# The end of a four-layer kernel: the last two chunks taken one by one instead of as a pair

## The chip, the cores and the metric

The kernel runs on one core of a Trainium2 chip. A core has TensorE (PE: matrix products and transposes, with its weight loads shown as PEld), VectorE (DVE), ScalarE (ACT), GpSimd (POOL), and SyncE (SP), which issues transfers. Each engine works through its own queue in order, and engines wait for one another through semaphores. PE writes its results to PSUM, eight banks of 512 floats in each of 128 partitions; the other engines copy them from there to SBUF. The metric is the device time in microseconds (us) of one execution.

## The reference

A stream x of 32 batches x 128 positions x 128 features goes through four blocks, each added to the stream: an attention of 16 heads of 64, a gated recurrence with a small coupling network, an attention of 16 heads of 8 behind a mixture of four experts (two chosen per batch), and last a slot network. The change is about this last block and about the end of the attention before it. Cut to what matters:

```python
out = attention(x) + x ; out = gamma * (out - mean) / sqrt(var + eps) + beta   # block 3, added to x
x1  = x + x @ layer_b                  # layer_b = base + rank-8 update of batch b
h   = gelu(x1 @ w1 + c)                # 128 -> 64 features
lg  = (h @ w2 + b2) / (|tau| + 0.1)    # 64 routes per position
alpha = softmax over the 8 highest of lg, 0 elsewhere
si  = alpha.T @ x1 / alpha.sum()       # 64 slots per batch
r, z, n = gates(si, slot_init) ; S = (1 - z) * n + z * slot_init
y   = layernorm(S + softmax(q(S) k(S).T) v(S))
x   = x + alpha @ (y @ wvp) @ wo
```

gelu here is the exact one; the gates use tanh.

## The kernel before, in words

The stream is held transposed in one SBUF tile X: features in partitions, 4096 positions in columns. A chunk is four batches (512 columns); there are eight chunks, 0 to 7, in four pairs. `col(g)` is chunk g of X.

Blocks 3 and 4 are written out by hand as a line of numbered steps (lines 1475 to 1508). Pair r has 24 steps of experts (k = 0 to 23) and then 8 of attention, so a pair takes TURN = 32 steps, and all four end at step 128 (END). Attention is itself a pipeline over batches: `advance` (line 1415) issues in one step the masks and scores of a batch, the weights of the batch before, the transposes of the one before that, and so on, so that a batch's result is added to R three steps after it came in, and its moments are taken four steps after. The last batch of chunk 6 comes in at step 122, that of chunk 7 at step 126; three further calls of `advance`, at steps 128 to 130, drain the pipeline.

Beside this line runs a plan. `at(i, f, *args)` (line 1343) enters a function for step i; `steps(i)` (line 1466) first takes every running generator one `yield` further, in the order in which they were started, and then starts what is planned for i. The block-4 functions for chunk g, with the number of steps that each runs over, are:

- `after_attention(g)` (1111, five steps): normalisation of R on ACT, transposes, X with gamma added; the product with lw (the per-batch layer) and xc = X + that product; for the second chunk of a pair the hidden product of both chunks into one PSUM bank (chunk a in partitions 0 to 63, chunk c in 64 to 127); and xn, the transpose of xc.
- `hidden(r)` (1147): one gelu over the pair's 128 partitions. `routes_top(g)` (1152): the w2 product, the logits lg and their eight highest on DVE. `routes_exp(r)` (1170): the exps of both chunks.
- `routes(g)` (1175, three steps): alpha, the slot inputs, their transposes. `slots_new(g)` (1210, six steps): gates with two tanh, the new slots sn, queries and keys, values, scores. `slots_exp(r)` (1263): the exps of the scores of both chunks.
- `slots_told(g)` (1267, eight steps): the slot attention's transposes, its weighted sum y, the normalisation of y, the transposes of y and the copy yT, the product with wvo, and the product with alpha that is added to ot, a transposed copy of `col(g)`; ot then goes to the output by a transfer on SP's queue (line 1331).

A pair's plan starts at t, the first step after its attention: `after_attention` at t and t + 3, `hidden` at t + 7, `routes_top` at t + 8 and t + 9, and so on to `slots_told` at t + 37 and t + 39, so the slots of a pair are told a full turn later, during the experts' steps of a following pair. For pair 3 (chunks 6 and 7) t is 128 and nothing else is left to run beside it except the telling of pair 2 (chunks 4 and 5), at steps 133 and 135.

What sets the order of instructions: `act(...)` (line 378) pins every ScalarE instruction behind all that is traced before it, so ScalarE keeps the order of the steps. PE, DVE and POOL instructions are pinned in the same way only inside `advance` (which, up to step 127, also calls `steps`); elsewhere a planner in the compiler orders them by when it reckons them ready, with the order of the steps as priority.

Two small supplies matter. From block 3 on, `ps()` (line 294) hands out only the three PSUM banks of the ring marked C; a bank is free again when its last reader is done. And ot, lw and the like share two buffers of 256 KB (tag h1): `layer_made(3)` puts the lw of chunks 6 and 7 there at step 116, and each is free after its product in `after_attention`.

## Time and profile before

| | |
|---|---|
| median of 3 runs | 1285.85 us (1284.26 to 1286.2) |
| profiled execution, own time | 1289.78 us |
| its span | 1288.0 us |
| its mean granted PE clock | 0.938 |
| PE, DVE, ACT, POOL busy | 88, 58, 57, 38 % |

The profile is of one execution. A row of a group tells busy time, mean length in nanoseconds and the idle time just before, with what ended it. A row of the timeline begins with its start in us from the start of the span and its length. Short instructions of one engine overlap a little, so lengths can add up to more than the time from first to last. The granted clock (PEclk) is a share of full speed; PE's own lengths follow it.

The end in numbers, from the timeline: chunk 7's last attention result is added to R until 1203.4; its X is ready at 1211.0 and its xc at 1213.9; the pair's gelu ends at 1219.2, the exps of both chunks' routes at 1236.9, chunk 7's new slots at 1257.5, and the last addition to ot at 1284.6. Chunks 4 and 5 have their last additions at 1230.5 and 1239.0, chunk 6 at 1278.9.

### The profile page before, as it was taken

The page shows a single profiled execution, that of the slowest core. Times are in us where ns is not written, and L with a number is a line of the kernel's source. Part 1 is how long each engine was busy: PE and PEld are TensorE (multiplying, and loading weights), DVE is VectorE, ACT ScalarE, POOL GpSimd, SP SyncE. Part 2 cuts the span into 40 slices and gives each one's busy share as a digit, 9 for nine tenths or more (in the row PEclk, how much of TensorE's full clock was granted, in tenths as well). Part 3 has the DMA queues.
Part 4 walks back from the last instruction along what each step waited for, and adds up shares of the span by engine and source line. Part 5 has one row for each costly group of instructions (what it writes and reads, how often), then busy time and mean ns, then how long its engine had stood idle before and what let it go on. Part 6 is the DMA issues. An engine that isn't in the chain of part 4 may idle for free. (4 is left out here: it accounts for less than half of the span.)

```text
span 1288.0 us, 24292 instructions
## 1 busy us (share of the span) xinstructions
PE 1131.8 (88%) x9509; PEld 714.9 (56%) x9509; DVE 749.1 (58%) x1996; ACT 738.3 (57%) x1857; POOL 490.2 (38%) x433
## 2 busy tenths in 40 slices
PE   4999899989999899899887777998999899989765
PEld 1565555535555355555454445676776677667543
DVE  1354848465584655936736468555756674667454
ACT  1756565655656656554355555665875587558421
POOL 1555655446555555534345532123213321222000
PEclk9999999999999999889888898999999999999765
DMA  6000000000000000000231210144023502220000
GB/s 259 1 1 2 1 2 1 1 1 1 1 1 1 1 1 2 1 1 1 93 113 53 84 57 10 41 134 132 11 75 92 155 11 75 91 65 11 2 17 17
DMA packets 18322, 51.99 MB, mean 40 GB/s; under 512 B 1568, under 2 KB 7840, under 8 KB 17952
## 3 DMA queue, kind: packets, MB, share of 16 engines
q0 software_dynamic: 9648, 40.01, 10.0%
q1 hardware_dynamic: 7984, 9.38, 2.3%
q8 instruction: 75, 1.23, 0.4%
q10 hardware_dynamic: 576, 1.05, 0.2%
q14 instruction: 39, 0.32, 0.1%
HBM read 46.25 MB, written 2.10 MB: 38 GB/s over the span
## 5 line engine op out<-in xcount | busy, mean ns | idle before, releaser
L380 ACT ACTIVATE s_sb<-ps,s_max 128x128 f32<-128x128 f32 x512 | 139.2, 383 | 132.3 <-DVE s_max L256 125.9
L256 POOL TENSOR_TENSOR s_sb<-s_sb,s_sum 128x1024 f32<-128x1024 f32 (+1 forms) x64 | 119.7, 1871 | 76.7 <-DVE s_sum L256 58.0
L256 PE MATMUL ps<-hT,w_attn 128*128 128x512 f32 x256 | 126.6, 625 | 11.2 <-DVE hT L256 11.2
L256 POOL TENSOR_TENSOR s_half<-s_sb 128x512 f32<-128x512 f32 x62 | 79.5, 1282 | 110.6 <-ACT s_sb L380 110.5
L256 POOL DMA_INDIRECT ew<-in_expert,rows x64 | 64.4, 1006 | 127.4 <-DVE ye L256 79.4
L380 ACT ACTIVATE qk<-ps 128x512 f32<-128x512 f32 x128 | 74.4, 615 | 64.2 <-PE ps L256 63.7
L256 DVE TENSOR_REDUCE s_max<-ps 128x4 f32<-128x512 f32 x128 | 81.2, 673 | 51.1 <-PE ps L256 51.0
L380 ACT ACT_TABLE_LOAD x61 | 78.3, 1283 | 53.4 <-DVE s_max L256 38.9
L256 DVE TENSOR_REDUCE s_sum<-s_half 128x8 f32<-128x256 f32 x62 | 25.7, 415 | 121.8 <-POOL s_half L256 121.8
L256 PEld LDWEIGHTS ps<-qk 64*128 64x128 f32 x1024 | 66.9, 193 | 38.0 <-issue 38.0
L256 PEld LDWEIGHTS ps<-hT,w_attn 128*128 128x128 f32 x256 | 47.9, 197 | 71.4 <-issue 49.1
L380 ACT ACTIVATE he<-ps,ew 128x128 f32<-128x128 f32 x256 | 71.3, 386 | 26.3 <-issue 19.2
L380 ACT ACTIVATE s<-ps,s1max 128x128 f32<-128x128 f32 x256 | 73.1, 390 | 19.3 <-DVE s1max L256 19.3
L256 PEld LDWEIGHTS ps<-he,ew 128*128 128x128 f32 x512 | 68.2, 198 | 26.3 <-ACT he L380 14.2
L256 PE MATMUL ps<-he,ew 128*128 128x128 f32 x512 | 77.1, 292 | 6.2 <-ACT he L380 5.2
L256 PE MATMUL ps<-qk 64*128 64x128 f32 x1024 | 80.4, 292 | 0.0
L256 PE MATMUL ps<-w_base,s_sb 128*128 128x128 f32 x512 | 75.0, 291 | 3.6 <-ACT s_sb L380 2.7
L256 PE MATMUL ps<-pT,v 128*64 128x128 f32 x1024 | 73.0, 287 | 5.2 <-DVE X L256 2.5
L256 PE MATMUL ps<-X,ew 128*128 128x128 f32 x512 | 76.1, 282 | 0.4 <-DMA ew<-in_expert,rows 0.4
L256 DVE TENSOR_REDUCE s1m<-ps 128x6 f32<-128x384 f32 x128 | 64.9, 547 | 17.6 <-PE ps L256 17.6
L256 PEld LDWEIGHTS ps<-X,ew 128*128 128x128 f32 x512 | 66.7, 193 | 10.6 <-issue 9.0
L256 PE MATMUL ps<-w_base,s 128*128 128x128 f32 x384 | 62.2, 288 | 7.9 <-ACT s L380 4.8
(298 smaller groups left out, 2427.5 us busy)
## 6 DMA issues: line engine op xcount, KB each, us to landing
v1o<-v SPq DMA_DIRECT2D x8, 256.0 KB, 3.5
out_x<-ot SPq DMA_DIRECT2D x8, 256.0 KB, 2.3
X<-in_xT ACTq DMA_DIRECT2D x4, 256.0 KB, 7.0
X<-in_xT SPq DMA_DIRECT2D x4, 256.0 KB, 9.4
w_attn<-in_attn POOLq DMA_DIRECT2D x1, 1024.0 KB
w_lowr<-in_lowr SPq DMA_DIRECT2D x1, 1024.0 KB, 12.6
ew<-in_expert,rows POOLq DMA_INDIRECT x64, 5.4
w_ffn<-in_ffn SPq DMA_DIRECT2D x1, 928.0 KB, 10.5
```

The costliest lines, as they stand in the source:

```text
L256: ins = f(*args, **kwargs)
L380: return tc.keep_in_program_order(A.activation(*args, **kwargs))
```

## The change

Three things are changed in the plan and two functions get a form for one chunk.

1. Pair 3 is planned chunk by chunk. Chunk 6 starts at step 126 and chunk 7 at step 130, and each runs on its own: `after_attention(g, True)` makes the hidden product of that chunk alone in partitions 0 to 63, `hidden_alone` takes its gelu, and the later functions follow at +6 (`routes_top`), +7, +8, +11, +16 and +17 (`slots_told`). Chunk 6's `slots_told` so begins at step 143 and chunk 7's at 147, where they began at 165 and 167.
2. The telling of pair 2 begins at step 127 for chunk 4 and 131 for chunk 5, where it began at 133 and 135. The telling of pairs 0 and 1 keeps its steps.
3. In `slots_told`, for every chunk, the four transposes of the stream and their copy to ot stand ahead of the weighted sum, three `yield`s before the transposes of y, behind which they stood.

`routes_exp` and `slots_exp` take chunks instead of a pair. Nothing is computed differently but for the split gelu.

```diff
-    def after_attention(g):
+    def after_attention(g, alone=False):
...
-        if g % 2:
+        if alone:
+            HSs[g, 0] = ps()
+            mm(HSs[g, 0][:NS], w("f_w1a"), xc)
+        elif g % 2:
             HSs[g // 2] = ps()
...
+    def hidden_alone(g):
+        p = HSs[g, 0]
+        HSs[g, 0] = mpool.tile([P, CH], F32, tag="h2", name="hs", bufs=1)
+        act(HSs[g, 0][:NS], p[:NS], AF.Gelu, bias=cb1[:NS])
...
     def routes_top(g):
-        e = slice(g % 2 * NS, g % 2 * NS + NS)
-        hs = HSs[g // 2]
+        alone = (g, 0) in HSs
+        e = slice(0, NS) if alone else slice(g % 2 * NS, g % 2 * NS + NS)
+        hs = HSs[g, 0] if alone else HSs[g // 2]
...
-    def routes_exp(r):
-        for g in (2 * r, 2 * r + 1):
+    def routes_exp(*gs):
+        for g in gs:
...
-    def slots_exp(r):
-        for g in (2 * r, 2 * r + 1):
+    def slots_exp(*gs):
+        for g in gs:
...
         act(y, p[:, 2 * D :].rearrange("p (q d) -> p q d", d=D), AF.Copy)
         yield
+
+        ot = mpool.tile([P, CB, D], F32, tag="h1", name="ot")
+        p4 = ps()
+        for b in range(CB):
+            T.transpose(p4[:, bass.ts(b, S)], col(g)[:, bass.ts(b, S)], ident)
+        act(ot, b3(p4), AF.Copy)
         p = ps()
...
             T.transpose(p[:, bass.ts(q, P)], y[:, q, :], ident)
-
-        ot = mpool.tile([P, CB, D], F32, tag="h1", name="ot")
-        p4 = ps()
-        for b in range(CB):
-            T.transpose(p4[:, bass.ts(b, S)], col(g)[:, bass.ts(b, S)], ident)
-        act(ot, b3(p4), AF.Copy)
...
+        if r == NP - 1:
+
+            for g, n in ((a, t - 2), (c, t + 2)):
+                at(n, after_attention, g, True)
+                at(n + 5, hidden_alone, g)
+                at(n + 6, routes_top, g)
+                at(n + 7, routes_exp, g)
+                at(n + 8, routes, g)
+                at(n + 11, slots_new, g)
+                at(n + 16, slots_exp, g)
+                at(n + 17, slots_told, g)
+            continue
...
-        at(t + 25, slots_exp, r)
-        at(t + TURN + 5, slots_told, a)
-        at(t + TURN + 7, slots_told, c)
+        at(t + 25, slots_exp, a, c)
+        t += TURN + 5 if r < NP - 2 else TURN - 1
+        at(t, slots_told, a)
+        at(t + (2 if r < NP - 2 else 4), slots_told, c)
```

More of the change, by code (lines that the diff above doesn't have):

```diff
@@ L1404, in program @@
         at(t + 9, routes_top, c)
-        at(t + 12, routes_exp, r)
+        at(t + 12, routes_exp, a, c)
         at(t + 13, routes, a)
```

## The prediction

> **What bounds the kernel now.** I read the page's slices first, then stretches of the end, then ScalarE's own order of instructions there, then the timeline around each of its waits.

> ```profile
> span 1288.0 us, 24292 instructions
> ...
> PE   4999899989999899899887777998999899989765
> ...
> PEclk9999999999999999889888898999999999999765
> ```

> TensorE (PE) is nearly full until the last three slices of 32.2 us. There it is 70, 60 and 50 per cent busy and its granted clock falls too. That is the only stretch the change works on in earnest. Cut at seven places of the timeline:

> ```profile
> core 0: us, PE busy (x) PEld busy (x) DVE busy (x) ACT busy (x) POOL busy (x), PEclk, DMA share, GB/s
> 1184.03:1189.42 5.39, 5.09 (x132) 3.93 (x128) 4.87 (x22) 4.64 (x13) 1.11 (x2) 1.00 0.01 3
> 1194.90:1203.46 8.56, 7.63 (x152) 5.85 (x150) 2.17 (x8) 5.16 (x11) 1.29 (x3) 0.80 0.01 3
> 1203.46:1213.86 10.40, 6.71 (x28) 4.87 (x28) 5.80 (x22) 2.13 (x5) 0.00 (x0) 0.61 0.00 1
> 1213.86:1219.16 5.30, 3.78 (x21) 1.56 (x20) 1.84 (x11) 3.21 (x5) 0.00 (x0) 0.80 0.00 0
> 1219.16:1236.91 17.75, 11.74 (x55) 9.47 (x56) 11.58 (x66) 4.75 (x9) 0.00 (x0) 0.51 0.05 16
> 1236.91:1257.54 20.63, 12.63 (x64) 7.80 (x64) 10.70 (x33) 4.45 (x11) 0.00 (x0) 0.67 0.05 14
> 1257.54:1288.00 30.46, 17.19 (x80) 10.85 (x80) 11.30 (x54) 4.83 (x12) 0.00 (x0) 0.50 0.06 17
> ```

> The first row is one full attention step (5.4 us, PE 94 per cent busy, full clock). The others are the end: attention draining (chunk 7's last result at 1203.4), chunk 7's xc, the gelu, both exps of the routes, chunk 7's new slots, and the output. No engine is full after 1203: it is a chain of hand-overs. ScalarE (ACT) keeps the order in which the code writes it, and two of its waits are that order alone:

> ```profile
> 1228.21 0.41 DVE L256 TENSOR_TENSOR lg<-lg,m 128x256 f32<-128x256 f32 x1
> ...
> 1233.83 0.60 ACT L380 ACTIVATE ot<-ps 128x512 f32<-128x512 f32 x1 [7.27 <-PE ps L256]
> 1234.32 0.56 ACT L380 ACTIVATE yT<-ps,w_base 128x256 f32<-128x256 f32 x1
> 1234.90 1.28 ACT L380 ACT_TABLE_LOAD   x1
> ...
> 1236.19 0.72 ACT L380 ACTIVATE lg<-lg 128x256 f32<-128x256 f32 x2
> ...
> 1250.45 0.48 DVE L256 SCALAR_TENSOR_TENSOR n<-ps,w_base,rz 128x256 f32<-128x256 f32 x1
> ...
> 1252.96 0.46 ACT L380 ACTIVATE slot_qk<-ps,w_base 32x256 f32<-32x256 f32 x1 [2.51 <-PE ps L256]
> 1254.85 0.46 ACT L380 ACTIVATE slot_qk<-ps,w_base 32x256 f32<-32x256 f32 x1 [1.42 <-PE ps L256]
> 1255.22 0.40 ACT L380 ACTIVATE n<-n 128x256 f32<-128x256 f32 x1
> ```

> Both logits are ready at 1228.6, but the exps stand behind chunk 5's ot and yT and begin at 1236.2: 7.6 us. Chunk 7's n is ready at 1250.9 and its tanh waits until 1255.2 behind chunk 6's queries and keys: 4.3 us.

> **The parts of the change.** I follow chunk 7, which ends last, with PE durations as they stand at half clock.

> *Drain.* In steps 126 to 129 ACT gets R of chunk 6 (1.64 us) and chunk 4's sl_pT and y (0.38 + 0.36) among its last attention work. ACT has idle gaps of 1.19, 0.42, 0.19 and 1.19 there, so I give this nothing; behind them in its queue stands attention's last copy oS. DVE gets chunk 4's three short normalisations (0.7 us in 1194.9 to 1203.4, where it is 2.17 of 8.56 busy), POOL the memset of xn, and POOL has no other work after 1203. PE gets chunk 6's R transposes (1.1) and chunk 4's four transposes (1.27) ahead of the last values, because attention's instructions are pinned behind all that is traced before them: +2.4 (0 if the gaps hold it, 3.5 if ACT's work sticks out).

> *Up to xc.* Traced ahead of it on PE: of chunk 6 the lw product 2.1, its own hidden product 1.0 (half of the pair's 1.98), xc transposes 1.1, w2 product 1.85; of chunk 4 stream transposes 1.1, weighted sum 1.12, y 0.69, wvo 1.23; of chunk 5 1.26. Together 11.45. The row of 10.40 us leaves 6.7 beside chunk 7's own R transposes and lw product (1.63 + 2.1), so 4.7 sticks out. Lower bound 0 (the planner puts it behind), upper 8.5 (only the 3.0 of others' work done there now is hidden). I take +4.7, as PE's order follows program order when several are ready.

> *To the gelu,* now 5.30. One hidden product less: -1.0. ACT now writes gelu(6), exp(6), gelu(7), exp(7): four tables in place of two. [...] Gelu(7) also stands behind alT of chunk 6: exp 0.38, products 1.35, transposes 0.69, copy 0.38 make 2.8, about half of it while chunk 7's xc is transposed: +1.4 (0 to 2.8). Behind this gelu stand yT of chunk 5 and siT of chunk 6, which then come late for chunk 5's output and chunk 6's gates, not for chunk 7. Together +3.0.

> *To the exp,* now 17.75. What is left: w2 product 1.85, one logit group on DVE 3.4 (0.48 + 4 x 0.52 + 2 x 0.42), chunk 5's normalisation in between 1.8, exp 0.38, no ot or yT left in front: 7.4, so **-10.3**. The table load is hidden behind the logits.

> Up to the exp: 2.4 + 4.7 + 3.0 - 10.3 = -0.2. The wait of 7.6 us is paid back before it is reached.

> *Exp to new slots,* now 20.63. Chunk 7's own path is alpha 1.35, product 1.13, division 0.75, transposes 0.66, copy 0.38, gates 1.13 + 0.4 + 0.63 + 0.85 + 0.42, slots 1.2, hand-overs 0.7: 9.6. Chunk 6, four steps ahead, puts its queries, keys and values before the gates (1.06 + 1.06 + 2.1) and about 1.0 of DVE: 14.8, so -5.8. The tanh no longer stands behind queries (4.3 of it).

> *New slots to the end,* now 27.1 to the last addition. The own path is 17.7. On top: chunk 6's stream transposes and weighted sum 2.2, its y, wvo and output products 3.1, own stream transposes 1.1, half of chunk 6's normalisation 1.8: 25.9, so -1.2. The stream's move is in this: now the copy to ot stands right before yT,

> ```profile
> 1279.73 0.60 ACT L380 ACTIVATE ot<-ps 128x512 f32<-128x512 f32 x1 [4.74 <-PE ps L256]
> 1280.22 0.56 ACT L380 ACTIVATE yT<-ps,w_base 128x256 f32<-128x256 f32 x1
> ```

> though y's transposes end at 1278.6: 1.6 us, gone in the new order. The tile ot is taken while both lw of pair 3 are alive in the same two buffers, so chunk 5's copy waits for chunk 7's lw product and exp(6) stands behind it. Nothing late: by the sum exp(6)'s logits come no sooner. The output DMA of chunks 4 and 5 moves with it; SP has nothing behind it (0.38 us each, landing in 2.3).

> *Left out so far.* ps() has three banks here. Chunk 7's hidden product holds one until its gelu ends, 8.2 us by the sum where the pair's held it 5.3 (1213.9 to 1219.2), and two serve the rest: +1.2 (0 to 2.9). Laying the same rows out in the old order ends 1.3 us short of the trace: +1.3.

> *The six earlier chunks* get only the stream's move, in stretches where PE is 95 to 99 per cent busy: the same four transposes and one copy of 0.6 us, three slots earlier. Nothing; at most 0.5 us a pair either way.

> **Sum:** -0.2 - 5.8 - 1.2 + 2.5 = -4.7 us. The profiled execution took 1289.78 (its span 1288.0 and 1.78 around it), 3.93 above the median of the runs; I take the difference off the median: 1285.85 - 4.7 = **1281.1 us**. A difference under 0.2 per cent (2.6 us) counts as none.

> **Rivals.**

> *Slower: ACT's order, chunk 7's gelu behind chunk 6's exp.* From chunk 6's last logit operation to the end of gelu(7) ACT's order needs table 1.28, exp 0.38, alpha 1.35, transposes 0.69, alT 0.38, table 1.28, gelu 0.69: 6.1. My sum puts that gelu at 1229.2, so it stands with the logits at 1223.1. Now the first are done at 1225.9 and share DVE with chunks 4 and 5. Break-even is 1227.8; at 1232 the kernel is 4.2 us slower: **1290**. For it: three chunks stand before them on PE. Against: R of chunk 6 can start 6 us sooner (1195.5 for 1201.4).

> *No difference:* the exp is no earlier, and chunk 6's work, four steps ahead, only changes places with its old self before chunk 7: **1285.5**. [...]

> [...]

> **How the numbers follow.** My sum (1279 to 1283.5 as its own range): 0.40; clock 0.18; no difference 0.20; slower 0.22. Of my case 0.36 lies beyond 0.2 per cent and 0.04 within; of no difference 0.01 falls out on the slow side: faster 0.54, same 0.23, slower 0.23. Of the clock case the part under 1272, of the slower one the part over 1291, is left out, under 2 in 10: 1272 to 1291.

> **What would show it.** Right: exp(6) straight after its own logits, without ot and yT of chunk 5 before it; four table loads after 1199; xc of chunk 7 some 7 us later than 1213.9; tanh of n within 0.3 us of its n; yT not behind ot at the very end. Wrong: attention's last result later than 1208; gelu(7) later than 1234; a granted clock above 0.7 from 1203 to 1240; PE waits for banks over 3 us; or a change of over 2 us before 1184.

## The result, and the profile after

The changed kernel takes **1275.28 us** (median of 4 runs, 1274.24 to 1276.74) against 1286.03 (1284.26 to 1286.23) for the kernel before: a ratio of 0.9923, 95% interval 0.9911 to 0.9936, so 8.2 to 11.4 us less. The forecast was 1281.1: the direction was right and the time lies inside the range of 1272 to 1291, but the gain is more than twice the forecast one. It lies outside the sum's own range of 1279 to 1283.5: the wide range holds it only because the 1274 us of the rival called clock, an estimate of mine, had pulled its lower end down. The profiled execution took 1274.46 us, 0.8 below its median, where that of before was 3.8 above its own.

First the page of the kernel after, its slices.

```profile
span 1272.7 us, 24291 instructions
...
PE   3999899989989899899887767899899989998774
...
PEclk9999999999999989989898989999999999999867
```

Up to the last three slices nothing is different in kind; the end goes from 7, 6, 5 tenths of PE to 7, 7, 4. Now the end, cut at the same events as before the change (a full attention step; attention's last result to chunk 7's xc; to the gelu's end; to chunk 7's exp; to its new slots; to the end of the span). The columns are the stretch, its length, each engine's busy time with the number of its instructions, the granted PE clock, and transfers.

```profile
core 0: us, PE busy (x) PEld busy (x) DVE busy (x) ACT busy (x) POOL busy (x), PEclk, DMA share, GB/s
1178.10:1183.47 5.37, 5.09 (x132) 3.94 (x128) 4.57 (x19) 4.64 (x13) 1.11 (x2) 1.00 0.01 3
...
1198.92:1213.12 14.20, 10.34 (x49) 7.92 (x48) 8.83 (x55) 5.90 (x11) 0.00 (x0) 0.67 0.01 2
1213.12:1222.07 8.95, 5.31 (x37) 2.96 (x36) 6.23 (x30) 5.24 (x8) 0.00 (x0) 0.88 0.09 29
1222.07:1228.86 6.79, 6.52 (x26) 5.03 (x26) 4.07 (x20) 2.42 (x5) 0.00 (x0) 0.58 0.00 0
1228.86:1245.86 17.00, 10.60 (x43) 5.52 (x42) 8.89 (x26) 3.78 (x10) 0.00 (x0) 0.67 0.05 16
1245.86:1272.70 26.84, 12.71 (x76) 8.80 (x76) 11.33 (x51) 4.83 (x11) 0.00 (x0) 0.69 0.07 20
```

The stretch to xc has grown from 10.40 to 14.20 us and the one to the gelu from 5.30 to 8.95; the one from the gelu to the exp has shrunk from 17.75 to 6.79. After it, 20.63 became 17.00 and 30.46 became 26.84. The sign of every stretch is the forecast's. ScalarE's own order shows why; this is its timeline in the kernel after (start, length, instruction, in brackets the wait before it).

```profile
1213.28 0.60 ACT L380 ACTIVATE ot<-ps 128x512 f32<-128x512 f32 x1 [4.90 <-PE ps L256]
1213.90 1.28 ACT L380 ACT_TABLE_LOAD   x1
1215.19 0.42 ACT L380 ACTIVATE lg<-lg 128x256 f32<-128x256 f32 x1
1216.56 0.60 ACT L380 ACTIVATE xn<-ps 128x512 f32<-128x512 f32 x1 [0.95 <-PE ps L256]
1219.69 0.38 ACT L380 ACTIVATE alT<-ps 128x256 f32<-128x256 f32 x1 [2.54 <-PE ps L256]
1220.09 1.28 ACT L380 ACT_TABLE_LOAD   x1
1221.39 0.68 ACT L380 ACTIVATE hs<-ps,cb 64x512 f32<-64x512 f32 x1
1221.97 0.55 ACT L380 ACTIVATE yT<-ps,w_base 128x256 f32<-128x256 f32 x1
1222.42 0.37 ACT L380 ACTIVATE siT<-ps 128x256 f32<-128x256 f32 x1
1222.81 1.28 ACT L380 ACT_TABLE_LOAD   x1
1228.44 0.42 ACT L380 ACTIVATE lg<-lg 128x256 f32<-128x256 f32 x1 [4.35 <-DVE lg L256]
...
1264.93 0.56 ACT L380 ACTIVATE yT<-ps,w_base 128x256 f32<-128x256 f32 x1 [5.61 <-PE ps L256]
```

The last step of each chunk's logits on DVE and, further on, chunk 7's n with its tanh:

```profile
1214.72 0.42 DVE L256 TENSOR_TENSOR lg<-lg,m 128x256 f32<-128x256 f32 x1
...
1227.99 0.41 DVE L256 TENSOR_TENSOR lg<-lg,m 128x256 f32<-128x256 f32 x1
...
1243.41 0.48 DVE L256 SCALAR_TENSOR_TENSOR n<-ps,w_base,rz 128x256 f32<-128x256 f32 x1
...
1243.93 0.42 ACT L380 ACTIVATE n<-n 128x256 f32<-128x256 f32 x1 [0.89 <-DVE n L256]
```

And ScalarE's group of table loads after 1193.6 (line, engine, operation, count; busy, mean ns; idle before):

```profile
L380 ACT ACT_TABLE_LOAD x4 | 5.1, 1283 | 0.1
```

The same row of before, after 1199, from which the forecast took 2.57 us for two more loads:

```profile
L380 ACT ACT_TABLE_LOAD x2 | 2.6, 1283 | 0.0
```

Each exp now begins as soon as its own logits are there: chunk 6's at 1215.19 (logits done at 1215.14), chunk 7's at 1228.44 (1228.40). The ot and yT of chunk 5 have not left ScalarE's order: its ot still stands right ahead of chunk 6's exp, as the prediction said of the tile ot, and its yT ahead of chunk 7's. But both are done before those logits are. Chunk 6's table load ends 0.04 us after its logits, chunk 7's long before; in the kernel before, the exps began 7.6 us after both logits were ready. Chunk 7's gelu (hs at 1221.39) stands behind chunk 6's alT and a table load. At the very end yT waits for PE alone. The loads are four, with next to no idle time ahead of them.

The two profiled executions do not begin the end at the same time: attention's last transfer of v1o is issued at 1168.0 before and 1162.1 after, though 2.7 of these 5.9 us are there at the first one (702.0 and 699.3), before any changed instruction. I therefore count everything below from that last transfer. From it to the end of the span it is **120.0 us before and 110.6 after, 9.4 less**, which the interval above holds.

### The profile page after: what moved, and what is told of

Its sections match the earlier page's. It is cut to its first block, busy times and chain, and to the rows that moved or that the text cites. A ratio compares the mean times of both kernels' runs of the same rounds, so it can differ in the third digit from the quotient of the medians.

```text
span 1272.7 us, 24291 instructions
## 1 busy us (share of the span) xinstructions
PE 1119.8 (88%) x9509; PEld 708.1 (56%) x9509; DVE 749.9 (59%) x1996; ACT 741.9 (58%) x1860; POOL 488.6 (38%) x433
## 3 DMA queue, kind: packets, MB, share of 16 engines
q8 instruction: 75, 1.23, 0.4%
## 5 line engine op out<-in xcount | busy, mean ns | idle before, releaser
L380 ACT ACTIVATE s_sb<-ps,s_max 128x128 f32<-128x128 f32 x512 | 139.2, 383 | 132.6 <-DVE s_max L256 126.3
L256 POOL TENSOR_TENSOR s_sb<-s_sb,s_sum 128x1024 f32<-128x1024 f32 (+1 forms) x64 | 119.7, 1871 | 76.6 <-DVE s_sum L256 58.0
L256 PE MATMUL ps<-hT,w_attn 128*128 128x512 f32 x256 | 126.4, 623 | 11.7 <-DVE hT L256 11.3
L256 POOL TENSOR_TENSOR s_half<-s_sb 128x512 f32<-128x512 f32 x62 | 79.5, 1282 | 108.5 <-ACT s_sb L380 108.4
L256 POOL DMA_INDIRECT ew<-in_expert,rows x64 | 63.5, 992 | 129.2 <-DVE ye L256 79.3
L380 ACT ACT_TABLE_LOAD x63 | 80.8, 1283 | 52.5 <-DVE s_max L256 38.9
L380 ACT ACTIVATE qk<-ps 128x512 f32<-128x512 f32 x128 | 74.4, 616 | 61.5 <-PE ps L256 60.9
L256 DVE TENSOR_REDUCE s_max<-ps 128x4 f32<-128x512 f32 x128 | 81.1, 673 | 48.2 <-PE ps L256 48.0
L256 DVE TENSOR_REDUCE s_sum<-s_half 128x8 f32<-128x256 f32 x62 | 25.7, 415 | 122.1 <-POOL s_half L256 122.1
L380 ACT ACTIVATE he<-ps,ew 128x128 f32<-128x128 f32 x256 | 71.6, 385 | 32.3 <-issue 19.0
L256 PEld LDWEIGHTS ps<-hT,w_attn 128*128 128x128 f32 x256 | 47.5, 196 | 71.7 <-issue 48.4
L256 PEld LDWEIGHTS ps<-qk 64*128 64x128 f32 x1024 | 66.2, 190 | 36.9 <-issue 36.9
L380 ACT ACTIVATE s<-ps,s1max 128x128 f32<-128x128 f32 x256 | 73.1, 390 | 19.7 <-DVE s1max L256 19.6
L256 PE MATMUL ps<-he,ew 128*128 128x128 f32 x512 | 76.3, 289 | 5.4 <-ACT he L380 4.6
L256 PEld LDWEIGHTS ps<-he,ew 128*128 128x128 f32 x512 | 67.1, 195 | 24.3 <-ACT he L380 12.4
L256 PE MATMUL ps<-qk 64*128 64x128 f32 x1024 | 79.6, 289 | 0.0
L256 PE MATMUL ps<-pT,v 128*64 128x128 f32 x1024 | 72.7, 286 | 5.3 <-DVE X L256 2.5
L256 PE MATMUL ps<-w_base,s_sb 128*128 128x128 f32 x512 | 74.2, 289 | 3.6 <-ACT s_sb L380 2.7
L256 PE MATMUL ps<-X,ew 128*128 128x128 f32 x512 | 76.6, 281 | 0.4 <-DMA ew<-in_expert,rows 0.4
L256 DVE TENSOR_REDUCE s1m<-ps 128x6 f32<-128x384 f32 x128 | 64.9, 547 | 16.3 <-PE ps L256 16.3
L256 PEld LDWEIGHTS ps<-X,ew 128*128 128x128 f32 x512 | 66.8, 192 | 10.9 <-issue 9.2
L256 PE MATMUL ps<-w_base,s 128*128 128x128 f32 x384 | 62.1, 288 | 7.9 <-ACT s L380 4.8
```

The costliest lines, as they stand in the source:

```text
L256: ins = f(*args, **kwargs)
L380: return tc.keep_in_program_order(A.activation(*args, **kwargs))
```

## The experiments

The theory after the result: it is the change of order, with exps that no longer wait for chunk 5 as its core. Rivals: PE's clock (0.50 in the last stretch before, 0.69 after), or one part alone, or something ahead of the end.

**The parts by themselves.** e1 does only the move of the stream's transposes and ot. e2 does only the earlier telling of chunks 4 and 5:

```diff
-        at(t + TURN + 5, slots_told, a)
-        at(t + TURN + 7, slots_told, c)
+        t += TURN + 5 if r != NP - 2 else TURN - 1
+        at(t, slots_told, a)
+        at(t + (2 if r != NP - 2 else 4), slots_told, c)
```

e3 is the changed kernel with ot's four transposes and copy put back:

```diff
         yield
-        ot = mpool.tile([P, CB, D], F32, tag="h1", name="ot")
-        p4 = ps()
-        for b in range(CB):
-            T.transpose(p4[:, bass.ts(b, S)], col(g)[:, bass.ts(b, S)], ident)
-        act(ot, b3(p4), AF.Copy)
         p = ps()
...
             T.transpose(p[:, bass.ts(q, P)], y[:, q, :], ident)
+        ot = mpool.tile([P, CB, D], F32, tag="h1", name="ot")
+        p4 = ps()
+        for b in range(CB):
+            T.transpose(p4[:, bass.ts(b, S)], col(g)[:, bass.ts(b, S)], ident)
+        act(ot, b3(p4), AF.Copy)
```

> Only the stream's transposes and the copy to ot go two steps sooner; the last pair stays together and slots_told stay at their old steps. My account: at the very end ot no longer stands right before yT (1.6 us between the end of y's transposes and yT's start in the profile of before), but chunk 5's ot still stands with yT before the exps, so about 1284.3 us, -1.6 us. If the tile ot makes the early copy wait for chunk 7's lw product and exp behind it, 1285 to 1288. If the move changes the six earlier chunks (1.4 us of the whole gain lie outside the last stretch in the two medians), 1282.9 or less with the first changed attention step already earlier in the trace. If it is off the path, 1285.9.

> Only slots_told of chunks 4 and 5 go into the attention's drain (steps 127 and 131); the last pair stays together and the stream's transposes stay where they were. My account: ot and yT of chunk 5 are gone from in front of the exps (7.6 us), while PE gets four to five us of their work ahead of chunk 7's xc: about 1282.5 us, -3.4. If this part carries the whole gain and the split only changes places, 1276 to 1278. If the work only shifts in front of xc one for one, 1285.9. With the exps 7.6 us sooner and nothing paid, 1278.3.

> The whole change without its last part: the stream's transposes and the copy to ot are back after y's transposes, right before yT. My account: ot before yT costs 1.6 us at the end of chunk 7, so 1276.9 us (1.6 above the changed kernel). If the early copy to ot made exp(6) wait for its tile, the time is equal to or under the changed kernel's 1275.3. If the stream's move gave nothing, 1275.3.

| kernel | ratio to before, 95% | last v1o to end | change | last stretch (new slots to last addition), its clock |
|---|---|---|---|---|
| before | 1 | 120.0 | | 27.10, 0.50 |
| e1, stream alone | 0.9966 (0.9951 to 0.9981) | 117.6 | -2.4 | 24.84, 0.50 |
| e2, telling alone | 0.9963 (0.9949 to 0.9977) | 116.9 | -3.1 | 27.07, 0.50 |
| e3, all but the stream | 0.9939 (0.9923 to 0.9956) | 113.9 | -6.1 | 26.45, 0.50 |
| after | 0.9923 (0.9911 to 0.9936) | 110.6 | -9.4 | 23.49, 0.72 |

No part carries it alone: telling gives 3.1, the split on top of it 3.0 (6.1 less 3.1), the stream on top of both 3.3 (9.4 less 6.1), or 2.4 by itself. The split without the earlier telling was not tried. A trace shows one execution, and those of before, e1, e2 and e3 took 2 to 3.8 us more than their medians. By the ratios e1, e2 and e3 gain more, 4.4, 4.8 and 7.8 us of the whole 9.9; the stream's move on top of the rest, 2.1 by them, is not clear of noise. By either count no single part makes the whole.

e2 shows the exps by themselves, and what the split is for. With the pair together and only the telling earlier, chunk 5's ot and yT stand in a stretch in which the logits are not ready, and each exp waits for DVE:

```profile
1222.12 0.59 ACT L380 ACTIVATE ot<-ps 128x512 f32<-128x512 f32 x1
1222.60 0.57 ACT L380 ACTIVATE yT<-ps,w_base 128x256 f32<-128x256 f32 x1
...
1227.47 0.42 ACT L380 ACTIVATE lg<-lg 128x256 f32<-128x256 f32 x1 [3.01 <-DVE lg L256]
1230.11 0.42 ACT L380 ACTIVATE lg<-lg 128x256 f32<-128x256 f32 x1 [2.22 <-DVE lg L256]
```

The exps end at 63.2 and 65.8 us from the last v1o transfer (before: 68.9 for the later), but chunk 7's new slots come only 3.1 us sooner. From its exp to its new slots it takes 20.65 us, as before (20.63), where e3 with the split takes 16.61: together, both chunks go through the gates side by side.

e1 gave 2.4 in its trace where I had expected 1.6, e2 3.1 where I had expected 3.4, and what e3 lacks reads 3.3, again for 1.6. Of these, e1's is the clean one, because the last stretch ran at the same clock in both kernels. These are the rows of that stretch, first before, then e1:

```profile
1257.54:1284.64 27.10, 17.19 (x80) 10.85 (x80) 11.30 (x54) 4.83 (x12) 0.00 (x0) 0.50 0.03 10
```

```profile
1254.39:1279.23 24.84, 16.85 (x80) 11.07 (x80) 11.22 (x54) 5.05 (x12) 0.00 (x0) 0.50 0.03 11
```

and these of e3 and of e10 (below), whose last stretch has the changed kernel's order:

```profile
1252.44:1278.89 26.45, 15.55 (x76) 10.52 (x76) 11.44 (x51) 4.52 (x11) 0.00 (x0) 0.50 0.04 11
```

```profile
1244.93:1270.59 25.66, 14.81 (x76) 9.80 (x76) 11.44 (x51) 4.85 (x11) 0.00 (x0) 0.57 0.04 11
```

At 0.57 the new order takes 25.66 (25.62 and 25.69 in e11 and e4, also at 0.57) against 23.49 at 0.72. So of the 3.0 us between e3's 26.45 and the 23.49 after, some 2.2 go with the clock and at most 0.8 with ot's place, since 0.50 and 0.57 are not the same clock either.

**Is it the clock?** The means of the stretches above, 0.58 to 0.88, hide how the clock ran. Cut at its own steps, the kernel after shows this (same columns as before):

```profile
1207.28:1210.69 3.41, 3.41 (x15) 3.01 (x14) 0.48 (x1) 0.97 (x3) 0.00 (x0) 0.50 0.02 5
1210.69:1214.11 3.42, 3.42 (x20) 2.87 (x19) 2.73 (x15) 0.81 (x2) 0.00 (x0) 0.50 0.00 0
1214.11:1217.52 3.41, 2.41 (x16) 1.13 (x14) 3.03 (x14) 2.08 (x3) 0.00 (x0) 1.00 0.19 61
1217.52:1220.93 3.41, 1.83 (x14) 1.10 (x14) 2.86 (x16) 1.22 (x2) 0.00 (x0) 1.00 0.05 16
1220.93:1224.35 3.42, 2.31 (x10) 2.11 (x10) 0.23 (x1) 3.13 (x5) 0.00 (x0) 0.50 0.00 0
1224.35:1227.76 3.41, 3.41 (x16) 2.58 (x15) 2.75 (x17) 0.00 (x0) 0.00 (x0) 0.50 0.00 0
1227.76:1231.17 3.41, 0.91 (x6) 0.34 (x4) 3.30 (x10) 0.94 (x2) 0.00 (x0) 1.00 0.25 77
```

Here it is 1.00 or 0.50, for whole windows of 3.41 us. Half clock gave way to full at 1214.11 after two windows of half clock with PE full (3.42 of 3.42 us in the second), and at 1227.76 after one (3.41 of 3.41); the window at full clock from 1217.52, with 1.83 us busy, was followed by half. So I tried to hold it up, with products that nobody reads. e4 puts 16 ahead of y's transposes in the last two chunks:

```diff
+        if g >= NCH - 2:
+            spare = bank("A")
+            for _ in range(16):
+                mm(spare[:, 0 : 2 * P], ident16, twice16.rearrange("p u t -> p (u t)"))
```

> The changed kernel with 16 idle products (128x256, bf16, into a spare bank, nobody reads them) while y of chunks 6 and 7 is normalised, where PE waits 4.1 us each time. It tells what the granted clock is worth: the end runs at 0.69 of full clock with PE 12.7 us busy of 26.9. If the low clock follows from PE's pauses and prices the end, 0.69 goes to 0.85 or more behind the filler and PE's own 12.7 us shrink by 2 us: 1273.3. If the clock does not answer to so short a filler, or its products reach past the wait: 1275.3 to 1277.

The ratio is 0.9932 (0.9909 to 0.9956), no different from the changed kernel. The products did not stay where I wrote them. They read only constants, nothing pins them, and the trace has all 32 between 1189.8 and 1203.7, in attention's drain. There they held the clock at 1.00, and chunk 7's xc stands at 49.3 us from the last v1o transfer in place of 51.0, but the last stretch ran at 0.57. The run says nothing of idle products at the end. e6 and e7 pin them, and spread them over the waits:

```diff
+    def idle(n):
+        if late:                       # from step 131
+            spare = bank("A")
+            pinned.append(True)
+            for _ in range(n):
+                mm(spare[:, 0 : 2 * P], ident16, twice16.rearrange("p u t -> p (u t)"))
+            pinned.pop()
...
+        idle(20)   # ahead of y's transposes; 10 ahead of xn's products and of sl_s's
+                   # transposes, 5 ahead of the w2 products and of the first slot products
```

e6 is this on the changed kernel, e7 on the kernel before; e5 is the changed kernel once more, beside them.

> The changed kernel once more, unchanged, beside the next three and enough executions of before to compare with runs 1 to 4. My account: 0.992 of before, as in the first measurement, with the same order of work. The clock's steps lie on a grid of 3.41 us in the six traces so far, and the grid stands differently to the work in each; if that alone makes the spread between executions, this trace shows the same order and waits, other places of the steps, and from the last copy of attention to the last addition something else than 72.4 us (0.71 of full clock).

> The changed kernel with idle products (128x256, bf16, nobody reads them), kept in their place by program order, right ahead of the products that PE waits for after step 130: 20 ahead of y's transposes, 10 ahead of the products of xn and of sl_s's transposes, 5 ahead of the first hidden and the first slot products. If PE's pauses hold the clock down and the clock prices the end: clock from the last copy of attention to the last addition from 0.71 to 0.9 or more, PE's own 47.4 us of products there shrink to about 37, some 60 per cent of that on the path, so 72.4 us become about 67 and the kernel takes 1270. If the clock is not what the end costs: 1275.5. If the idle products delay the real ones at half clock: up to 1279.

> The kernel before with the same idle products in the same places. With the clock high in both, what is left between this and e6_fill_after is the change of order alone. If the change gains by order (its 7.6 us of exps behind ot and yT, 1.6 us of ot before yT): e6 is 6 to 8 us faster than this. If the change gained mostly by a denser PE that gets more clock: e6 is within 3 us of this. Its own time by the first account about 1277, by the second 1272.

e5: 0.9922 (0.9905 to 0.9939), 1274.27 us. Its trace has the same order, 72.14 us from the last copy of attention to the last addition, and the clock's steps stand nearly as in the first trace, so it tells nothing about the spread between executions; that expectation was not borne out. e6: **0.9875** (0.9853 to 0.9896), 1267.0 us. e7: 0.9961 (0.9945 to 0.9977), 1278.6 us. From the last copy of attention to chunk 7's new slots and from there to the last addition, e6:

```profile
1195.44:1237.52 42.08, 34.81 (x268) 25.66 (x268) 28.67 (x131) 17.76 (x33) 0.45 (x1) 1.00 0.05 14
1237.52:1260.71 23.19, 17.37 (x127) 12.90 (x126) 11.32 (x51) 4.44 (x10) 0.00 (x0) 0.83 0.04 12
```

and e7:

```profile
1198.10:1251.42 53.32, 40.27 (x272) 28.97 (x272) 30.65 (x132) 16.07 (x33) 0.45 (x1) 0.87 0.04 11
1251.42:1273.83 22.41, 16.45 (x140) 12.00 (x140) 11.31 (x53) 4.84 (x12) 0.00 (x0) 0.98 0.04 12
```

The clock is high in both, though not quite the same (0.94 and 0.91 over both rows), and the difference stays: from the last v1o transfer to the end 103.5 against 112.5, **9.0 us**, where it was 9.4 without idle products and I had expected 6 to 8. The rival falls: the change gains by its order. The low clock is a cost of its own in either kernel: by the ratios to before, 6 us between e5 and e6 and 5 us between before and e7. In both, PE busy with work that nobody reads ended sooner than PE waiting.

The place of the gain is different with the clock held. In microseconds from the last v1o transfer:

| | before | after | change | e7 | e6 | change |
|---|---|---|---|---|---|---|
| last copy of attention | 33.5 | 34.9 | +1.4 | 33.4 | 34.9 | +1.5 |
| chunk 7's xc | 45.9 | 51.0 | +5.2 | 46.3 | 49.6 | +3.3 |
| its exp | 68.9 | 66.8 | -2.1 | 68.1 | 63.5 | -4.6 |
| its new slots | 89.5 | 83.8 | -5.8 | 86.7 | 77.0 | -9.7 |
| last addition | 116.6 | 107.3 | -9.4 | 109.1 | 100.2 | -8.9 |

With the clock held the whole 9 us are won by the new slots, 4.6 of them up to the exp, and the last stretch shows no gain (22.41 and 23.19), though e6 had the lower clock there (0.83 for 0.98). Without it, the lower clock in the packed stretch (0.73 after, from the last copy of attention to the exp; e6 has 1.00 up to the new slots) takes back part of this and a better clock at the end (0.72 for 0.50) returns it.

**The terms.** e8 gives the end all eight PSUM banks, e10 takes chunk 7's gelu ahead of chunk 6's alT, e11 takes the table loads of the end away:

```diff
         if i == END + 3:
+            short.clear()                          # e8
-                at(n + 5, hidden_alone, g)
+                at(n + 5 - g % 2, hidden_alone, g)   # e10
-        act(HSs[g, 0][:NS], p[:NS], AF.Gelu, bias=cb1[:NS])
+        act(HSs[g, 0][:NS], p[:NS], AF.Tanh, bias=cb1[:NS])   # e11
```

> The changed kernel with all eight PSUM banks for the work after step 130, where the change leaves it three (the other five are attention's). It measures the term of 1.2 us that I laid on the hidden product's bank. If the three banks hold the end up: 1274 or less, and PE's waits for banks go. If nothing waits for a bank: 1275.5, within 1 us of e5_again.

> The changed kernel with the gelu of chunk 7 one step sooner, so that ScalarE does it before chunk 6's alT; nothing else moves. In the changed kernel this gelu's products are done by 1215.9 and ScalarE has done chunk 6's exp and chunk 7's xn at 1217.2, but it waits for alT until 1219.7 and runs 1221.4 to 1222.1. If that order costs the end what I laid on it (1.4 us, at most 2.8): 1272.5 to 1274. If it costs all that the trace shows, from 1217.2 + 1.28 for the table to 1221.4: 2.9 us, 1271.5. If chunk 7's logits have to share DVE with chunk 5's normalisation anyway, or chunk 6's alT comes late by as much: 1275, no difference.

> The changed kernel with the function of the last pair's hidden units computed as tanh instead of gelu (so the routes of the last two chunks are other numbers; all sizes and waits are the same). Tanh stands in the table of the exp, so the four table loads of the end go. My sum laid 2.57 us on two more loads. If the loads stand on the path before both gelus: 1272.5. If only the load before chunk 7's gelu is on the path, with the others hidden behind the logits: about 1274. If all are hidden: 1275.3.

- e8: 0.9895 (0.9875 to 0.9915), 1270.25 us, some 3.5 us better than e5 by the ratios. So more banks are worth more here than my term of 1.2 (0 to 2.9). Whether PE waits for banks, or runs denser with more of them and so gets more clock, this run does not tell (e9 below). How much of it the split adds is open, since before was not run with eight banks.
- e10: 0.9926 (0.9909 to 0.9942), no gain. The gelu did come sooner: it ends at 58.3 us from the last v1o transfer for 59.8 in e5, chunk 7's exp at 65.5 for 66.6, its new slots at 81.3 for 83.6. Then the last stretch ran at 0.57 (the row above) and took 25.66 for e5's 23.39.
- e11: 0.9916 (0.9899 to 0.9934), again no gain to measure, though its trace has no table load left from 1193 to 1275: new slots at 81.8, last stretch 25.62 at 0.57. In e10 and e11 the clock at the end takes what the middle has gained, so neither prices its term.

e9 has the idle products and the eight banks; e12 adds e10's edit to it, to ask the same with the clock held.

> The changed kernel with both: the idle products of e6 and the eight banks of e8. If bank waits and clock are two separate costs of the end: the gains add, 7 and 4 us, about 1263.5. If the eight banks gained by letting PE run denser and so get more clock, or if the waits on DVE for y (8.4 us in e8) bound what is left: 1266 to 1267, no better than e6.

> e9 (idle products and eight banks) with the gelu of chunk 7 ahead of chunk 6's alT, as in e10, but now with the clock held: in e10 chunk 7's exp came 1.1 us sooner, and the last stretch then ran at half clock nearly throughout. In e9 ScalarE has done chunk 7's xn at 1218.8 and begins this gelu only at 1223.5, behind alT and its own table load; ahead of alT it could begin at 1220.1. If that order is a cost of the end: 2 to 3.4 us off e9, 1265 to 1266.5, and the trace from the last v1o transfer to the end 98 instead of 100.8. If chunk 7's logits then wait for DVE, or chunk 6's alT is late by as much: 1268.5, 100.8.

e9: 0.9863 (0.9842 to 0.9883), 1268.5 us. The gains of 6 us (e6) and 3.5 us (e8) would add to 9.5; the ratio gives 7.6 over e5, and the intervals are too wide to tell the two apart. Up to the new slots e9 stands where e6 does (77.2 and 77.0); what it has over e6 is in the last stretch, 20.35 us at 0.99 for 23.19 at 0.83. So with the clock held three banks are hardly a limit up to there, which speaks for the denser PE as what the banks bring in e8. e12: **0.9831** (0.9803 to 0.9859), 1263.3 us, the best of all. ScalarE's timeline around chunk 7's gelu in e9:

```profile
1218.16 0.60 ACT L380 ACTIVATE xn<-ps 128x512 f32<-128x512 f32 x1 [0.36 <-PE ps L256]
1221.81 0.38 ACT L380 ACTIVATE alT<-ps 128x256 f32<-128x256 f32 x1 [3.06 <-PE ps L256]
1222.21 1.28 ACT L380 ACT_TABLE_LOAD   x1
1223.51 0.68 ACT L380 ACTIVATE hs<-ps,cb 64x512 f32<-64x512 f32 x1
...
1229.75 0.42 ACT L380 ACTIVATE lg<-lg 128x256 f32<-128x256 f32 x1 [3.33 <-DVE lg L256]
```

and in e12 (the last v1o transfer is 3.7 us sooner here, 1162.4 for 1166.1):

```profile
1213.74 0.60 ACT L380 ACTIVATE xn<-ps 128x512 f32<-128x512 f32 x1 [0.36 <-PE ps L256]
1214.36 1.28 ACT L380 ACT_TABLE_LOAD   x1
1215.65 0.68 ACT L380 ACTIVATE hs<-ps,cb 64x512 f32<-64x512 f32 x1
1217.39 0.38 ACT L380 ACTIVATE alT<-ps 128x256 f32<-128x256 f32 x1 [1.05 <-PE ps L256]
...
1225.32 0.42 ACT L380 ACTIVATE lg<-lg 128x256 f32<-128x256 f32 x1 [3.32 <-DVE lg L256]
```

Counted from that transfer the gelu is 4.2 us sooner, the exp 0.7, the new slots 1.7, and the last stretch is the same 20.35. The whole is 1.6 us (99.2 for 100.8). By the ratios it could be more, but their intervals overlap. Behind the gelu PE did not use all of the lead. Its w2 products for chunk 7 start at 1220.45, behind y's transposes and 25 idle products of mine, so a better place for these might give more; that was not tried.

## Why the prediction was right, and where its size was off

The mechanism held and the sum came out 4.7 us where the trace has 9.4. Point by point, the size measured in the two profiles against that of the sum:

- *Drain, +2.4:* +1.4 to attention's last result. Right within its range.
- *Up to xc, +4.7:* +3.8. Three chunks' work does stand ahead of chunk 7's xc on PE. I had priced it throughout at half-clock lengths, and PE had full clock until 1203.9, for the first 5 of these 14.2 us.
- *To the gelu, +3.0:* +3.65. Of the 3.0, 2.57 stood for two more table loads, from the row of before; the four loads after took 1283 ns each, as that row has it. One of the four, that before chunk 7's exp, is hidden behind DVE's logits, as forecast (1224.1 for 1228.4). The wait behind alT, put at 1.4 with 0 to 2.8, is 1.6 by the traces of e12 and e9.
- *Gelu to exp, -10.3:* -10.96. This core term is right, and e2 and the timeline show its cause. Of the sign named for it the half came that counts: exp(6) follows its logits, with chunk 5's ot still ahead of it.
- *Exp to new slots, -5.8:* -3.6 after, -5.1 with the clock held. The work named is there: chunk 6's queries, keys and values stand on PE from 1235.3 to 1239.4, ahead of chunk 7's gates. Tanh of chunk 7's n follows its n at once (1243.93, n done at 1243.89). But chunk 6's own tanh waited from 1230.8 to 1233.3 behind alT of chunk 7, a wait I had not written down.
- *New slots to the end, -1.2:* **-3.6. This step failed.** Its shape is right (ot is gone from before yT; e1 gives 2.3 us in this stretch for it at equal clock, where I had 1.6), but I took half clock for granted there. The stretch had 0.72, and at 0.57 the same order takes 25.6 to 25.7, which is -1.4 to -1.5.
- *Banks +1.2 and shortfall +1.3:* these 2.5 us were added on top of a sum of rows, but the stretches measured already hold all the time from the last v1o transfer to the last addition. Whatever the banks cost lies inside them, and two of them came out 2.85 us worse than their terms. So whether the allowances were needless, or were right and were spent there, is not shown: more banks gain 3.5 us in e8, next to nothing up to the new slots in e9, and the trace names no wait as one for a bank, so the sign I named (over 3 us of them) cannot be read from it. A shortfall found when laying out the old order says what that layout lacks, not that the new order will lack it too. Without the two the sum is -7.2.

Together, with nothing set against the allowances: 2.5 for them, 2.4 for the last stretch, 1.9 for drain and xc, and 0.66 for gelu to exp make 7.5 too cautious; exp to new slots (2.2) and the way to the gelu (0.65) were too hopeful by 2.85. The difference, 4.6, is the miss but for rounding.

*The rivals.* Slower: its deciding point, chunk 6's logits at 1227.8, came at 1215.1 (1221.0 in the time of before), so ScalarE's order never got to it. No difference: falls with the exp, sooner by 2.1. The clock, with its chance of 0.18: the 1274 was my estimate that two thirds of some 22 us of PE work from 1203 to 1237 would take half the time. No run shows that: after the change the rows up to the exp have 0.67, 0.88 and 0.58. The 1275.3 is near it, but not by its cause, since 9.0 us stay with the clock held in both. Where I was wrong is in reading means: I took the 0.80 from 1213.86 to 1219.16 and the 0.51 from there to 1236.91, with PE 66 per cent busy, as if each were the clock of the whole row. Cut on the clock's own grid, the trace of before shows what they were:

```profile
1212.54:1215.95 3.41, 3.41 (x12) 1.40 (x12) 0.69 (x1) 0.65 (x2) 0.00 (x0) 0.50 0.00 0
1215.95:1219.37 3.41, 1.89 (x17) 1.29 (x18) 2.01 (x12) 2.61 (x4) 0.00 (x0) 1.00 0.00 0
1219.37:1222.78 3.41, 3.41 (x20) 2.96 (x20) 1.83 (x11) 0.60 (x2) 0.00 (x0) 0.50 0.02 5
1222.78:1226.19 3.41, 2.69 (x12) 2.17 (x11) 3.41 (x24) 0.69 (x2) 0.00 (x0) 0.50 0.00 0
```

The 0.80 was a mean of 0.50 and 1.00. The 0.51 was half clock from 1219.37 on, with PE full only in the first window. A full window did not always bring full clock: the one from 1212.54 was followed by 1.00, the one from 1219.37 by 0.50. The rows should have been cut into single windows. Then the waits would have been priced as costs in themselves, of which the idle products show the size: 5 us between before and e7, by the ratios. That the time came so near to 1274 is luck. The sign I named for it, a clock above 0.7 from 1203 to 1240, did not come (0.65).

*The sign before 1184.* I had named a change of over 2 us before that as a refutation; it is 5.9. In e2 and e3, which change nothing before step 126, the last v1o transfer is issued at 1164.7 and 1168.3, and over all fourteen traces at 1160.5 to 1168.3, so most of it is the spread between executions. From the first v1o transfer to the last, the ten kernels with the stream's move take 463.8 us on average (462.3 to 466.4) and the four without it 466.1 (463.6 to 468.9). Up to 2 us may thus be gained in the earlier pairs, where I had at most 0.5 a pair. This stays open, as does why the medians of the first measurement differ by 10.75 and the end by 9.4.

## What to carry to other kernels

In a tail where no engine is full, ask which instruction of another chunk stands ahead of the critical one in an engine's fixed order, and move that work into an earlier stretch with gaps; here the wait that went was worth more than the work that was added (11.0 us from the gelu to the exp, against 7.45 from attention's last result to the gelu). Do not carry PE's lengths from one clock state over to another (the eight lw products of a chunk took 1.16 us at 1.00 and 2.08 at 0.50, both in the trace of before): cut the trace at the clock's own steps, and count a pause of PE twice, once as a wait and once as the slower window behind it (it followed 48 of 50 windows at full clock that had PE busy under 50 per cent, as counted below). An edit that gains in the middle can read as nothing because the next stretch ran at another clock (e10, e11), so hold the clock before deciding on small edits.

## What the runs showed that I had not expected

Neither the change nor its neighbours are the end of it: e12, the changed kernel with pinned idle products, all eight banks after step 130 and chunk 7's gelu ahead of chunk 6's alT, takes 1263.3 us, 1.7 per cent under the kernel before and 0.9 per cent under the changed one.
